# Gated cross-attention and a fake-quantised FFN on one core: the place of four weight chunks in VectorE's order, the queue of the raw up stores, and the place of one half of transposes

## The chip, the core and the metric

The kernel runs on one NeuronCore of a Trainium2 chip. Its engines work side by side, each through its own instructions in a fixed order: TensorE (PE: matmuls and transposes, with its weight loads shown as PEld), VectorE (DVE), ScalarE (ACT), GpSimd (POOL) and SyncE (SP, which only issues DMAs here). DMAs are issued through the queue of SP, ACT or POOL and are moved by 16 DMA engines. An instruction starts when it is at the head of its engine and what it waits for (semaphores) has happened.

The metric is the device time of one execution in microseconds (us). Before the change the median of three runs is 1495.26 us (1495.17 to 1497.37).

## The reference, cut to what matters

`x` has 4 x 1024 tokens of 512 channels, `ctx` 4 x 64 tokens. A layer norm and a cross-attention with 16 heads of 64 come first, then a layer norm and an FFN of width 1536, whose weights are quantised to 4 bits in blocks of 32 and whose activations are quantised to 16 bits with one scale for the whole tensor.

```python
x = x + jnp.tanh(g_xattn[0]) * xattn(_layernorm(x), ctx_1024, ctx_1024, w_q, w_k, w_v, w_o)
x = x + jnp.tanh(g_ffn[0]) * ffn(_layernorm(x), w_gate, w_up, w_down)

def ffn(x, w_gate, w_up, w_down):
    x = act_qdq(x)                          # 16 bits, one maximum over the whole tensor
    up = act_qdq(x @ lpbq_dequant(w_up).T)  # 4-bit weights, a scale for each block of 32
    gate = act_qdq(x @ lpbq_dequant(w_gate).T)
    sig = fixed_qdq_u16(jax.nn.sigmoid(gate))
    gate = act_qdq(gate * sig)
    o = act_qdq(gate * up)
    return o @ lpbq_dequant(w_down).T
```

Each `act_qdq` needs the maximum of a whole tensor before a single element can be rounded, so the FFN is cut into stages: all gate products, all up products, then the down products. Raw gate and raw up values go to memory in between.

## The kernel before, in words

**Stages.** (1) *Setup* (to about 95 us): the context is turned and multiplied with `w_k` and `w_v`, and `w_q`, `w_o` are folded in, so that attention needs only two products for each token tile: scores against `m_all`, weights against `vwo`. (2) *Attention* (95 to 580 us): 16 pairs of token tiles of 128. (3) *Gate products* (585 to 880 us), 24 units. (4) *Up products* (873 to 1180 us), 24 units. (5) *Down products* and output (1190 us to the end). The large products use Strassen's scheme: seven products m1 to m7 in place of eight, with the sums made on DVE and by accumulation in PSUM.

**Who sets the order.** In attention and in the gate and up stages PE runs in the order in which the code is written (`tc.manual_schedule`). The other engines' instructions are ordered by a planner from modelled costs; `tc.high_priority(SOON)` lets an instruction be drawn ahead, and `tc.keep_in_program_order(ins)` holds an instruction at its place in the code relative to others held so. An instruction that is not held may be placed far ahead of its place in the code.

**Setup.** `query_turned(hp)` turns `w_q` on PE (L443) and copies the result to `wqT` on DVE (L447). The products `ps_m` (L465) read `wqT`; their results are copied to `m_all` by ACT (L476) and DVE (L478). SP loads `c_sb`, `wk_sb`, `wq_sb`, `wv_sb`, `wo_sb`, the first token group `xg` and then four chunks `w_g`, in that order.

**Gate weights.** `dequantized` (L207 to L219) loads a chunk of 128 x 512, finds the largest magnitude of each block of 32 (L212, `wam`), makes scale and inverse (L213, L215), multiplies, rounds and multiplies back (L217, L218, L219). The twelve gate chunks are dequantised in the attention loop, each three tiles ahead (`AHEAD`) of the tile `gate_at` at which PE turns it (L224) inside `between`; the tile `wraw` has four buffers.

**Attention.** For pair q, `scores(q + 1)` and `softmax(q + 1)` are written first, then `attend(t)` for the two tiles of pair q. `softmax` runs 16 exponentials for each tile on ACT (L590) and normalises on DVE (L595, L596). `attend` turns the softmax tile in two halves of four transposes (L610, into PSUM `ps_e`), which ACT copies to `eT` (L612), calls `between` (a turned `xm` tile of an earlier group, L640, and at twelve tiles a gate chunk), then runs eight products `po` (L616): the first four read the first half of `eT`, the last four the second. `ps_e`, `ps_xm`, `ps_xn` and the turned weight chunks share the PSUM pool `ps_tr` of three buffers.

**Up stage.** Seven products of four matmul records each make a unit. `interleaved` sets PE's order to m1, m7 of the unit before, m5, m4 of the unit before, m2, m3 of the unit before, m6. m1 and m2 accumulate in the same PSUM bank `pp`: ACT must copy m1's result out (L766) before m2 may start, and m2's (L774) later. DVE takes the other results out (L779, L784, L944). `raw_up` has four buffers, two for each unit (`r0`, `r1`), so `r0` of a unit can be written only when the store of `r0` two units before has landed. `up_done` takes the maximum (L952) and stores the half unit to `up_d` (L956). ACT also makes the gate integers (L986, L987, L989) and magnitudes (L1018) there, DVE the products with them (L996, L1019).

Of the kernel before, what the change touches and what calls it, by code (L numbers as in the profile page):

```python
# [12 lines left out]
ALU = mybir.AluOpType  # L13
AX = mybir.AxisListType
# [3 lines left out]
P = 128  # L18
# [9 lines left out]
def kernel(  # L28
# [39 lines left out]
    nc = tc.nc  # L68
# [8 lines left out]
    TPB = S // P  # L77
# [12 lines left out]
    GRP = 4  # L90
# [113 lines left out]
            nc.vector.tensor_scalar(inv, inv, unit, None, ALU.mult)  # L204
        return s, inv

    def dequantized(pool, src, w, name):  # L207

        nc.sync.dma_start(out=w, in_=src)
        wb = w.rearrange("p (n k) -> p n k", k=QB)  # L210
        am = pool.tile([P, NQB], F32, name=f"wam_{name}", tag="wam")
        nc.vector.tensor_reduce(am, wb, AX.X, ALU.max, apply_absolute_value=True)  # L212
        nc.vector.tensor_scalar(am, am, 1.0 / W_QMAX, 1e-12, ALU.mult, ALU.max)  # L213
        inv = pool.tile([P, NQB], F32, name=f"winv_{name}", tag="winv")
        nc.vector.reciprocal(inv, am)  # L215
        shape = [P, NQB, QB]
        nc.vector.tensor_tensor(wb, wb, inv.unsqueeze(2).to_broadcast(shape), ALU.mult)  # L217
        nc.vector.tensor_scalar(w, w, MAGIC, MAGIC, ALU.add, ALU.subtract)  # L218
        nc.vector.tensor_tensor(wb, wb, am.unsqueeze(2).to_broadcast(shape), ALU.mult)  # L219
# [9 lines left out]
    wgT, wuT, wd, wdT, up_chunks = [], [], [], [], []  # L229

    def turned_chunk(psp, w, oc, into, name):

        if oc % 4 == 0:
            into.append(slot([P, HC, 4 * P], f"w{name}T{oc // 4}"))
        cols = slice((oc % 4) * P, (oc % 4 + 1) * P)
        ps = psp.tile([P, 4, P], F32, name=f"wps_{name}{oc}", tag="tr")
        turned(ps, w, into[-1][:, :, cols])
# [71 lines left out]
    pa = pools.enter_context(tc.tile_pool(name="pa", bufs=2))  # L309
    ps_tr = pools.enter_context(tc.tile_pool(name="ps_tr", bufs=3, space=PSUM))  # L310
# [52 lines left out]
    with tc.tile_pool(name="su", bufs=1) as su, tc.tile_pool(  # L363
        name="ps_mm", bufs=5, space=PSUM
# [7 lines left out]
        for k in range(P // BL):  # L372
            w = slice(k * BL, (k + 1) * BL)
# [77 lines left out]
        for hp in range(HP):  # L451
# [4 lines left out]
            for h2 in range(HC // 2):  # L456
# [13 lines left out]
                for j in range(2):  # L470
                    for b in range(B):
                        at = (hp % 4) * P + (j if b % 2 == 0 else 1 - j) * D
                        dst = m_all[b][hp // 4][:, 2 * h2 : 2 * h2 + 2, at : at + D]
                        src = two[j][:, :, b * KL : (b + 1) * KL]
# [43 lines left out]
    with tc.tile_pool(name="ps_s", bufs=1, space=PSUM) as ps_s, tc.tile_pool(  # L518
# [48 lines left out]
        def softmax(q, e):  # L567

            for i in range(2):
                t = 2 * q + i  # L570
                ei = e[:, i]

                if t % TPB == 0:
                    nc.vector.tensor_tensor(
                        ei, ei, cmask.unsqueeze(1).to_broadcast([P, NH, KL]), ALU.add
                    )
                mx = pa.tile([P, NH], F32, name=f"mx{t}", tag="mx")
                nc.vector.tensor_reduce(mx, ei, AX.X, ALU.max)
                sm = pa.tile([P, NH], F32, name=f"sm{t}", tag="sm")
                if q == 0:  # L580

                    nc.vector.tensor_tensor(
                        ei, ei, mx.unsqueeze(2).to_broadcast([P, NH, KL]), ALU.subtract
                    )
                    nc.scalar.activation(ei, ei, AF.Exp)
                    nc.vector.tensor_reduce(sm, ei, AX.X, ALU.add)
                else:
                    nc.vector.tensor_scalar(mx, mx, -1.0, None, ALU.mult)  # L588
                    for h in range(NH):
                        nc.scalar.activation(  # L590
                            ei[:, h, :], ei[:, h, :], AF.Exp, bias=mx[:, h : h + 1],
                            accum_out=sm[:, h : h + 1],
                        )
                rs = pa.tile([P, NH], F32, name=f"rs{t}", tag="rs")
                nc.vector.reciprocal(rs, sm)  # L595
                nc.vector.tensor_tensor(  # L596
                    ei, ei, rs.unsqueeze(2).to_broadcast([P, NH, KL]), ALU.mult
                )

        def attend(t, e, then):  # L600

            b = t // TPB
            g, i = divmod(t, GRP)
            ef = e[:, t % 2].rearrange("p h k -> p (h k)")
            eT = pa.tile([P, HP, P], F32, name=f"eT{t}", tag="eT")
            for q in range(HP // 4):
                ps = ps_tr.tile([P, 4, P], F32, name=f"ps_e{t}_{q}", tag="tr")
                for j in range(4):
                    hp = 4 * q + j
                    nc.tensor.transpose(ps[:, j, :], ef[:, hp * P : (hp + 1) * P], ident)  # L610
                with tc.high_priority(SOON):
                    nc.scalar.copy(eT[:, 4 * q : 4 * q + 4, :], ps)  # L612
            then()
            po = ps_o.tile([P, H], F32, name=f"po{t}", tag="po")
            for hp in range(HP):
                nc.tensor.matmul(  # L616
                    po, eT[:, hp, :], vwo[b][hp // 4][:, hp % 4, :],
                    start=(hp == 0), stop=(hp == HP - 1),
                )
            x1 = xg[g][:, i, :]  # L620
            with tc.high_priority(SOON):
                nc.vector.scalar_tensor_tensor(x1, po, tanh_g[0], x1, ALU.mult, ALU.add)
            nc.gpsimd.dma_start(out=x1_d[t], in_=x1)
            stats(pa, x1, mv2[:, t, :], f"b{t}")
# [30 lines left out]
        gate_raw = {}  # L655
# [10 lines left out]
        for q in range(NQ):  # L666
            b, k = divmod(q, QPB)
            e = ahead
            if q % 2 == 0 and q // 2 + 2 < NG:
                load_group(q // 2 + 2)  # L670

            if b + 1 < B:
                if b > 0 and k == 0:
                    fetched(m_all[b + 1], m_d[b + 1], f"mb{b + 1}")
                if b > 0 and k == QPB - 1:
                    fetched(vwo[b + 1], vwo_d[b + 1], f"vb{b + 1}")
                if k == 1:
                    sums_ahead = score_sums(b + 1)
                if k in (1, 2):
                    next(sums_ahead)  # L680
            if q + 2 < NQ:
                two = centred(q + 2)
            if q + 1 < NQ:
                ahead = scores(q + 1, lambda: next_left(q + 2))
                softmax(q + 1, ahead)
            for i in range(2):
                t = 2 * q + i

                def between():
                    if q > 1:  # L690
                        renormed(t - GRP)
                    if t in gate_at:
                        oc = gate_at.index(t)
                        turned_chunk(ps_tr, gate_raw.pop(oc), oc, wgT, "g")

                attend(t, e, between)
                if t + AHEAD in gate_at:
                    oc = gate_at.index(t + AHEAD)
                    w = pa.tile([P, H], F32, name=f"w_g{oc}", tag="wraw", bufs=4)
                    dequantized(pa, w_gate[oc * P : (oc + 1) * P, :], w, f"g{oc}")  # L700
                    gate_raw[oc] = w
                if t >= NT - UPB:
                    ag.append(weight_sums(wgT, sg_t, t - (NT - UPB), "g"))

                if t >= last - GRP:
                    oc = t - (last - GRP)
                    if oc % GRP == 0:
                        w4 = slot([P, GRP, H], f"w_eu{oc // GRP}")
                    w = w4[:, oc % GRP, :]
                    dequantized(pa, w_up[oc * P : (oc + 1) * P, :], w, f"eu{oc}")  # L710
                    early_up.append(w)
                for c, d in ((0, 2), (2, 3), (3, 4)):
                    if t == last + d - 1:
                        w = slice(last + c, last + d)
                        rstd_of(pa, [(rstd2[:, w], mv2[:, w, 1])], f"c{c}")
            if q % 2 == 1 and q + 1 < NQ:
                g = q // 2
                parts = [(rstd2[:, of_group(g)], mv2[:, of_group(g), 1])]
                if g + 2 < NG:
                    group_stats(pa, g + 2)  # L720
                    parts.append((rstd1[:, of_group(g + 2)], mv1[:, of_group(g + 2), 1]))
                rstd_of(pa, parts, f"b{g}")
# [12 lines left out]
    with tc.tile_pool(name="praw", bufs=RAW) as praw, tc.tile_pool(  # L735
# [184 lines left out]
        with tc.tile_pool(name="pc", bufs=2) as pc, tc.tile_pool(  # L920
# [27 lines left out]
            def up_done(r, v, k):  # L948
                u = unit_of(v, k)
                raw[u] = r.rearrange("p i n -> p (i n)")  # L950
                if v != order[-1]:
                    nc.vector.tensor_reduce(  # L952
                        am_up[:, u : u + 1], raw[u], AX.X, ALU.max, apply_absolute_value=True
                    )
                queue = nc.sync if v == order[-1] else nc.scalar
                queue.dma_start(out=up_d[u], in_=raw[u])  # L956


# [462 lines left out]
```

## Time and profile before

| | |
|---|---|
| median of three runs | 1495.26 us |
| the profiled execution: its time / its span | 1494.27 us / 1492.5 us |
| PE busy | 1444.5 us, 97% of the span |
| DVE, ACT, POOL busy | 1087.2, 635.6, 70.5 us |
| PE, one product of the up stage (two matmuls of 512 columns, four records) | starts every 1.72 us |
| raw up stores, 46 of 512 KB through ACT's queue (L956) | 338 ns of the queue each, landing after 2.6 / 4.9 / 8.5 us (least, median, most) |

The page lists busy time by engine, the span in 40 slices, the DMA queues, the chain of work that ended last, the costliest groups of instructions, and the DMA issues. The trace behind it answers for a stretch of time: what ran (the timeline, with the idle time ahead of an instruction and what ended it in brackets), who waited for whom, and busy time by window. A duration is in us in the timeline and in ns in lists by line; "x4" counts records.

### The profile page before, as it was taken

The numbers are of one execution on the slowest core, as the hardware profiler recorded it, in microseconds if no ns is written. First come the engines' busy times: TensorE is split into PE (matmuls) and PEld (weight loads), VectorE is DVE, ScalarE is ACT, GpSimd is POOL, SyncE is SP. The second block draws the span as 40 slices with busy tenths as digits, with TensorE's granted clock in tenths as the row PEclk, the third lists the DMA queues.
The fourth block names the chain that finished last, engine by engine and source line by source line (L and its number), as shares of the span: only waits on it lengthen the run. The fifth ranks groups of instructions, "written<-read, shape, count | busy, mean of one in ns | idle before, by whom it ended". The sixth has DMA issues, their size and how long they took to land. (4 is left out here: it accounts for less than half of the span.)

```text
span 1492.5 us, 14450 instructions
## 1 busy us (share of the span) xinstructions
PE 1444.5 (97%) x4656; PEld 795.4 (53%) x4656; DVE 1087.2 (73%) x1986; ACT 635.6 (43%) x1653; POOL 70.5 (5%) x143
## 2 busy tenths in 40 slices
PE   5999999999999999999999999999998899999999
PEld 4734444455445445444444444444443448888887
DVE  2777657567686978999855558888887897666642
ACT  0435566456655664110000127777789532222200
POOL 0000000000000001000000000000000101111110
PEclk8999999999999999999999999999999999999999
DMA  8250202311221234743322528858575485555321
GB/s 295 86 226 15 98 22 100 108 69 53 75 106 64 71 134 162 281 169 155 127 84 85 175 93 310 333 198 324 208 288 210 181 306 206 183 183 170 141 71 43
DMA packets 71475, 231.66 MB, mean 155 GB/s; under 512 B 7268, under 2 KB 7524, under 8 KB 65892
## 3 DMA queue, kind: packets, MB, share of 16 engines
q1 hardware_dynamic: 46212, 131.09, 24.7%
q0 software_dynamic: 11648, 50.34, 8.8%
q10 hardware_dynamic: 13536, 49.29, 8.3%
q8 instruction: 36, 0.59, 0.2%
q14 instruction: 43, 0.35, 0.1%
HBM read 123.74 MB, written 106.95 MB: 155 GB/s over the span
## 5 line engine op out<-in xcount | busy, mean ns | idle before, releaser
L590 ACT ACTIVATE e<-e,mx 128x64 f32<-128x64 f32 x480 | 159.6, 337 | 17.9 <-DVE mx L588 17.8
L616 PE MATMUL po<-vwo,eT 128*128 128x512 f32 x256 | 114.1, 599 | 2.3 <-ACT eT L612 2.0
L616 PE MATMUL po<-vb,eT 128*128 128x512 f32 x256 | 112.9, 594 | 0.8 <-ACT eT L612 0.8
L758 PE MATMUL pqup<-t,wuT 128*128 128x512 f32 x192 | 92.1, 602 | 2.2 <-DVE raw_up L779 1.7
L590 ACT ACTIVATION_READ_ACCUMULATOR e<-e,mx 128x1 f32 x480 | 91.6, 191 | 0.0
L758 PE MATMUL pqgate<-t,wgT 128*128 128x512 f32 x192 | 90.4, 593 | 0.0
L616 PEld LDWEIGHTS po<-vwo,eT 128*128 128x128 f32 x256 | 47.3, 190 | 58.8 <-issue 53.6
L1287 PE MATMUL ep<-wdT,upe 128*128 128x256 f32 x336 | 77.1, 379 | 0.0
L774 ACT COPY raw_gate<-ppgate 128x512 f32<-128x512 f32 x24 | 14.0, 585 | 147.8 <-PE ppgate L758 147.8
L616 PEld LDWEIGHTS po<-vb,eT 128*128 128x128 f32 x256 | 47.4, 190 | 55.2 <-issue 53.6
L1213 ACT ACTIVATE uie<-upe,inv_up 128x1024 int16<-128x1024 f32 x48 | 53.6, 1144 | 50.5 <-DVE upe L1217 31.5
L1287 PE MATMUL eq<-tw,upe 128*128 128x256 f32 x312 | 72.6, 380 | 0.5 <-DVE c L1305 0.5
L758 PE MATMUL ppup<-xu,wuT 128*128 128x512 f32 x144 | 69.2, 604 | 4.0 <-ACT raw_up L766 4.0
L1287 PEld LDWEIGHTS ep<-wdT,upe 128*128 128x128 f32 x336 | 63.8, 190 | 9.1 <-issue 0.5
L758 PE MATMUL ppgate<-xh,wgT 128*128 128x512 f32 x144 | 67.7, 592 | 0.0
L1217 DVE SCALAR_TENSOR_TENSOR upe<-uie,inv_o,gse 128x1024 f32<-128x1024 int16 (+1 forms) x50 | 60.5, 1237 | 5.3 <-ACT uie L1213 5.3
L1287 PEld LDWEIGHTS eq<-tw,upe 128*128 128x128 f32 x312 | 59.1, 190 | 9.1 <-DVE c L1305 1.1
L540 DVE TENSOR_TENSOR e<-sq,e 128x512 f32<-128x512 f32 x48 | 33.1, 689 | 42.1 <-PE sq L534 42.0
L758 PEld LDWEIGHTS pqup<-t,wuT 128*128 128x128 f32 x192 | 34.9, 189 | 52.1 <-issue 34.0
L758 PEld LDWEIGHTS pqgate<-t,wgT 128*128 128x128 f32 x192 | 36.2, 190 | 46.4 <-issue 38.5
L996 DVE SCALAR_TENSOR_TENSOR q<-gi,inv_gs,si 128x1024 int16<-128x1024 int16 x44 | 55.7, 1277 | 4.8 <-ACT si L989 4.7
L886 DVE TENSOR_REDUCE am_gate<-raw_gate 128x1 f32<-128x1024 f32 x48 | 58.2, 1212 | 0.9
(329 smaller groups left out, 2845.9 us busy)
## 6 DMA issues: line engine op xcount, KB each, us to landing
gate_d<-raw_gate ACTq DMA_DIRECT2D x48, 512.0 KB, 2.6
gt<-gate_d SPq DMA_DIRECT2D x48, 512.0 KB, 6.0
upe<-up_d SPq DMA_DIRECT2D x24, 1024.0 KB, 6.5
up_d<-raw_up ACTq DMA_DIRECT2D x46, 512.0 KB, 5.0
gse<-gsi_d SPq DMA_DIRECT2D x24, 512.0 KB, 5.0
gsi_d<-q SPq DMA_DIRECT2D x44, 256.0 KB, 4.3
xg<-in_x_dram SPq DMA_DIRECT2D x8, 1024.0 KB, 6.4
x_d<-xg POOLq DMA_DIRECT2D x32, 256.0 KB, 2.3
```

The source lines that it names most:

```text
L540: nc.vector.tensor_tensor(dst, bank[at], other, add)
L590: nc.scalar.activation(ei[:, h, :], ei[:, h, :], AF.Exp, bias=mx[:, h : h + 1], accum_out=sm[:, h : h + 1],)
L616: nc.tensor.matmul(po, eT[:, hp, :], vwo[b][hp // 4][:, hp % 4, :], start=(hp == 0), stop=(hp == HP - 1),)
L758: nc.tensor.matmul(bank[at], a[k][:, h, :], b[k][:, h, :], start=start and h == 0, stop=h == HC // 2 - 1, skip_group_check=True,)
L774: nc.scalar.copy(r0[:, 0, :], bank["pp"])
L886: nc.vector.tensor_reduce(am_gate[:, u : u + 1], rf, AX.X, ALU.max, apply_absolute_value=True)
L996: nc.vector.scalar_tensor_tensor(gsi[u], gi, c_gs, si, ALU.mult, ALU.mult)
L1213: nc.scalar.activation(ui, up[:, i, :], AF.Copy, scale=inv_u)
L1217: ins = nc.vector.scalar_tensor_tensor(o[:, i, w], ui[:, w], c_o, gs[:, i, w], ALU.mult, ALU.mult)
L1287: nc.tensor.matmul(bank[at], a[u // 2][k][:, u % 2, q % 2, :], w_of[u // 2][k][:, u % 2, :], start=start and u == 0, stop=u == UPB - 1, sk ...
```

## The change

Three edits.

1. The first instruction (the reduction) of gate chunks 0 to 3 is held in program order in DVE's stream.
2. The stores of raw up go out through POOL's queue rather than ACT's; those of the last unit stay with SP.
3. `attend` is split. A generator `weights_turned` turns one half of a softmax tile per step. For a pair, the first half of the second tile is turned after `between`'s work of the first tile and in front of the first tile's products; its second half is turned where the whole tile was turned before.

```diff
-    def dequantized(pool, src, w, name):
+    def dequantized(pool, src, w, name, in_order=False):
...
-        nc.vector.tensor_reduce(am, wb, AX.X, ALU.max, apply_absolute_value=True)
+        ins = nc.vector.tensor_reduce(am, wb, AX.X, ALU.max, apply_absolute_value=True)
+        if in_order:
+            tc.keep_in_program_order(ins)
...
-        def attend(t, e, then):
-
-            b = t // TPB
-            g, i = divmod(t, GRP)
+        def weights_turned(t, e):
+
             ef = e[:, t % 2].rearrange("p h k -> p (h k)")
             eT = pa.tile([P, HP, P], F32, name=f"eT{t}", tag="eT")
             for q in range(HP // 4):
...
                 with tc.high_priority(SOON):
                     nc.scalar.copy(eT[:, 4 * q : 4 * q + 4, :], ps)
-            then()
+                yield eT
+
+        def attend(t, eT):
+
+            b = t // TPB
+            g, i = divmod(t, GRP)
             po = ps_o.tile([P, H], F32, name=f"po{t}", tag="po")
...
+            turns = [weights_turned(2 * q + i, e) for i in range(2)]
+            next(turns[0])
             for i in range(2):
                 t = 2 * q + i
-
-                def between():
-                    if q > 1:
-                        renormed(t - GRP)
-                    if t in gate_at:
-                        oc = gate_at.index(t)
-                        turned_chunk(ps_tr, gate_raw.pop(oc), oc, wgT, "g")
-
-                attend(t, e, between)
+                eT = next(turns[i])
+                if q > 1:
+                    renormed(t - GRP)
+                if t in gate_at:
+                    oc = gate_at.index(t)
+                    turned_chunk(ps_tr, gate_raw.pop(oc), oc, wgT, "g")
+                if i == 0:
+                    next(turns[1])
+                attend(t, eT)
...
-                    dequantized(pa, w_gate[oc * P : (oc + 1) * P, :], w, f"g{oc}")
+                    dequantized(pa, w_gate[oc * P : (oc + 1) * P, :], w, f"g{oc}", oc < 4)
...
-                queue = nc.sync if v == order[-1] else nc.scalar
+                queue = nc.sync if v == order[-1] else nc.gpsimd
```

Because the planner places everything that is not held, the three edits also change the order of many other DVE, ACT and SP instructions in attention and in the up stage. PE's order changes only by the moved transposes.

## The prediction

> **What bounds the kernel now.** First the page: PE is busy 1444.5 of 1492.5 us. A faster DVE, ACT or queue is worth only the 48 us in which PE stands still, or runs slowly after it. So I read who PE waited for, longest first (engine, line, releaser: us in all, times, longest):
>
> ```profile
> PE ps_m L465 <- DVE wqT L447: 15.4, 1, 15.4
> PE ps_c L413 <- DMA c_sb<-in_ctx_dram: 4.7, 1, 4.7
> PE ps_d L1364 <- DVE upe L1222: 4.5, 1, 4.5
> PE ppup L758 <- ACT raw_up L766: 4.0, 1, 4.0
> PE po L616 <- ACT eT L612: 2.8, 10, 0.5
> ```
>
> Rows 1, 4 and 5 are what the three edits touch. Row 1 is a single stop in the setup; the timelines of PE and DVE there show its cause (start, duration, in brackets the idle time before and who ended it):
>
> ```profile
> 23.87 1.04 PE L443 MATMUL ps_wq<-ident,wq_sb 128*128 128x128 f32 x8
> 40.31 3.48 PE L465 MATMUL ps_m<-kT,wqT 64*128 64x256 f32 x16 [15.40 <-DVE wqT L447]
> ...
> 44.30 2.00 PE L465 MATMUL ps_m<-kT,wqT 64*128 64x256 f32 x16
> ```
>
> ```profile
> 29.67 0.69 DVE L212 TENSOR_REDUCE wam_g<-w_g 128x16 f32<-128x512 f32 x1 [22.35 <-DMA w_g<-in_L_ffn_w_gate_dram]
> ...
> 38.87 0.69 DVE L219 TENSOR_TENSOR w_g<-w_g,wam_g 128x512 f32<-128x512 f32 x1
> 39.48 1.28 DVE L447 COPY wqT<-ps_wq 128x512 f32<-128x512 f32 x2
> ```
>
> PE has turned the first `wq` chunk at 24.4, but DVE is stuck at the head of its stream on gate chunk 0, last in SP's load order, until 29.67. It then works off four chunks, and only then copies `wqT`. The granted clock shows a second cost (windows: us, busy and count of PE, PEld, DVE, ACT, POOL, then clock, DMA share, GB/s):
>
> ```profile
> 25.00:40.00 15.00, 0.00 (x0) 0.00 (x0) 10.26 (x25) 0.00 (x0) 0.00 (x0) 0.66 0.42 154
> 40.00:42.00 2.00, 1.69 (x8) 1.56 (x10) 0.76 (x2) 0.00 (x0) 0.00 (x0) 0.50 0.00 0
> 50.00:60.00 10.00, 10.00 (x70) 8.01 (x70) 5.48 (x19) 4.25 (x18) 1.41 (x2) 1.00 0.38 117
> ```
>
> Row 4 is one stop in the up stage (PE, then ACT):
>
> ```profile
> 1122.43 1.88 PE L758 MATMUL pqup<-t,wuT 128*128 128x512 f32 x4
> 1128.26 3.30 PE L758 MATMUL ppup<-xu,wuT 128*128 128x512 f32 x4 [3.96 <-ACT raw_up L766]
> 1131.36 2.31 PE L758 MATMUL pnup<-b,su 128*128 128x512 f32 x4
> ```
>
> ```profile
> 1125.75 1.99 ACT L1018 ACTIVATE ar<-raw_up 128x1024 f32<-128x1024 f32 x2
> 1127.52 0.36 ACTq L956 DMA_DIRECT2D up_d<-raw_up  x1
> 1127.65 0.56 ACT L766 COPY raw_up<-ppup 128x512 f32<-128x512 f32 x1
> ```
>
> PE's next product needs a PSUM bank that ACT should have emptied; ACT is busy without a gap on other work that stands ahead of that copy.
>
> **Edit 1, the held chunks.** In the changed program's DVE order no gate instruction stands ahead of `wqT` any more; all 24 of them stand in attention. What was hidden behind PE's stop must now be early enough. `wqT` for the first head pair: transposes end at 24.4, copy 0.68 us, handover about 0.2 (as elsewhere between these engines), so `ps_m` starts near 25.3 instead of 40.31: **15.0 us**. The first 16 `ps_m` records took from 40.31 to 43.72, 3.41 us, the next 16 took 1.93 (44.30 to 46.23); with no stop the clock stays at 1.00: **1.5 us** more. Is anything else late at 25 us? By issue time plus landing time, `wv_sb` is there by 20.8, `wo_sb` by 26.2, `xg` by 28.9; they are needed at about 30, 61 and 46 on the new clock. The POOL stores and the SP load of the next `xg` hang on `m_all` and `wqT`, and move with them. So 16.5 us, between 15 and 17.
>
> The chunks' DVE work (29.67 to 39.48, 9.8 us in all) moves behind tiles 13, 14, 15 and 17, about 290 to 375 us. From 300 to 400 DVE is busy 71.06 us and PE 99.49, so it has 29 us per 100 to take it. In the densest place two chunks' reductions and small steps, 1.7 us, stand between a tile's statistics and the first `sq` sum. DVE comes free about 1.7 us after `po` ends, that makes 3.4, and `sq` is due 3.6 us after `po` ends (two products of 1.72). Between this sum and the next stand 3.2 us where 3.4 are free. PE would wait only from 1.7 us later still (the product on `sn` lies between). Loss between 0 and 3; I take **0.5**. Each chunk is turned three tiles, some 40 us, after its reduction. Their DMAs keep their place in SP's queue.
>
> **Edit 3, the half turn.** No transposes are added. It puts 0.43 us of PE work between the first tile's second half and its products, and lets the second tile's products start on a half that is long copied. Row 5 is what it can remove: 10 stops of 0.18 to 0.46, 2.8 us, and 0.2 at `wps_g`. It adds a wait: at the eight even tiles from 16 on with a gate chunk, the moved half is the fifth in a row through three `ps_tr` buffers and needs the second half's copy. In the pair at 391.82 this copy ends at 393.58 (392.51 + 1.07) and the fifth transposes would start at 393.6: 0.1 to 0.2 each, 1.2 us in all. Queued behind it on PE are the eight products. It also needs the second tile's weights 3.4 us earlier than before; tightest is the last pair, with no scores ahead: normalised by 561.9, needed at about 562.7. Net between -1 and +3; I take **2.0**.
>
> **Edit 2, the stores.** It frees 46 x 0.338 = 15.5 us of ACT's queue and, worth more, ACT no longer stands still for DVE's sums before it issues. How late the stores were: DVE finished a half unit at 1112.95 and ACT's queue issued at 1116.81; the next was finished at 1116.45 and issued at 1124.00. And ACT's copies waited for such stores to land: 13.3 us, 6 times. POOL has no other work from the gate maximum to the last unit. Ideal length of the up stage: from 873.00, 24 x 7 products of 1.7165 = 288.4, three products of the gate tail 5.1, two transposed chunks 0.9: 294.4. Last product's end 1179.3, so 306.3 were taken and **11.9 are lost**. Of these 5.8 are the stop above (3.96, and 1.4 + 0.4 in the two slow products after it), 1.2 one slip at 1043.6, the rest slips of 0.1 to 0.2 where DVE's L779 is late.
>
> Does the stop go? Before it, 12 large ACT instructions of about 1.05 us stood between m2's copy at 1114.05 and m1's copy at 1127.65. In the changed program ACT's order is nearly the same in every unit: five between m1's copy and m2's (5.0 us; PE leaves 6.9), three between m2's and the next m1's (3.1; PE leaves 5.2); at the ends of the stage at most six and five. ACT needs about 9 us and DVE 9.4 of a unit's 12.0. So the stop and the slip, 7.0 us, should go. The small slips are DVE's order, which I leave in. Bounds: -2 to +11.9; I take **7.0**.
>
> Here a rule speaks against the edit. **The Trainium skill ("SBUF — State Buffer", section "SBUF: two separate sides")** says that descriptors of POOL's DMAs can't be written while DVE runs in a 2-port mode. Its figure: 0.62 us alone, 3.1 when overlapped. The row first:
>
> ```profile
> L623 POOL DMA_DIRECT2D x_d<-xg x32: 542/542/547, 132.4 to 579.2; - x32
> L867 POOL DMA_DIRECT2D ts_d<-t x12: 533/533/819, 589.7 to 734.6; - x12
> ```
>
> Under a DVE busy to 70 to 85% an issue took 533 to 547 ns and once 819; 256 KB landed after 2.3 us, 512 KB after 2.9. By the row a store costs 0.54 us on an idle engine; by the rule 2.5 us more. The room: `r0` is complete about 7.9 us into the next unit, and m1's copy of the second unit after it wants the buffer at 13.9: 5.9 us, and 4.6 more before PE stops, since m2 comes 5.15 us after m1. With the median landing of 4.9 the row gives no PE stop, and the rule (7.4) blocks ACT for 1.5 us per unit, still without one. I take the row: no cost.
>
> **Sum.** 16.5 + 2.0 + 7.0 - 0.5 = 25.0. The profiled execution took 1494.27 (span 1492.5 and 1.8 around it): 1469.3. The median of the runs lies 1.0 above it. I say **1470**.
>
> **Rivals.** (a) *The up stage gives nothing*: the new order of ACT and DVE trades the one stop for others as long (ACT copies late behind `ar`, which waits for DVE). For it: the whole stage is reordered, and DVE at 83% already slips. Against: the even order. 1494.3 - 18.0 = 1476. (b) *The up stage runs clean* and edit 3 gives its whole: 16.5 + 3 + 11.9, about 1463. (c) *The chunks' DVE work lands on PE*: if all 9.8 us stalled the scores, 1469.3 + 9.3 = 1479; against it, the slack of 1.7 us per sum. (d) *Slower*: POOL's stores starve. The place is m1's copy behind `r0`'s store. PE loses what a landing takes over 10.5 us after DVE's sum. To eat the 18 us that the other edits give, 22 units must lose 0.8 us each: every store must land after 11.3 us, where 8.5 is the worst seen. (e) *The edits don't do what they say*: the hold would have to leave the chunks in front, and the order excludes it.
>
> **Chances.** Forecast 0.60 (1465 to 1474), (a) 0.18, (b) 0.09, (c) 0.07, (d) 0.03, (e) and mishaps unseen 0.03. The range 1462.5 to 1481 takes in (b), (a), (c). About 0.2% (3 us) is what a measurement of this kernel tells from no change: faster 0.94, the same 0.02, slower 0.04.
>
> **What the profile after would show.** Right: `ps_m` starts near 25.3 with the clock at 1.00 to 60 us, and everything to 590 us lies 16 to 19 us earlier; PE's list has no row `ps_m` <- `wqT` and hardly one `po` <- `eT`; ACT's wait for `up_d` nearly gone, no stop of over 1 us between the first up product and the last, and the stage 7 us shorter. Wrong: PE waits for `e` L540 at 290 to 375 us (c); for `raw_up` L766 or L779 in the up stage (a); POOL issues over 1 us and landings of 8 us or more (d). The rows after 1190 us should keep their lengths.

## The result, and the profile after

The changed kernel takes **1473.72 us** (median of four runs, 1472.88 to 1474.68) against 1495.36 beside it: ratio 0.9853, 95% interval 0.9835 to 0.987, so some 22 us faster. Its profiled execution took 1473.96 us with a span of 1472.1, that is 20.3 us less than the one before.

The list of PE's waits of the changed kernel, as shown of before (engine, line, releaser: us in all, times, longest). It leaves out idle times under 0.15 us:

```profile
PE ps_c L415 <- DMA c_sb<-in_ctx_dram: 4.7, 1, 4.7
PE ps_xn L335 <- DVE xn L323: 3.2, 2, 2.6
PE ps_d L1371 <- SPq L1193: 2.7, 1, 2.7
PE pqup L765 <- DVE raw_up L786: 2.1, 4, 0.7
...
PE pqup L765 <- DVE raw_up L791: 1.8, 3, 1.2
...
PE ps_e L610 <- DVE e L598: 1.7, 2, 1.1
```

The three rows that the edits aimed at are gone from the top: `ps_m` <- `wqT` (15.4), `ppup` <- `raw_up` (4.0), `po` <- `eT` (2.8). In their place stand small waits for DVE: the normed tile `xn`, the sums of m6 (L786) and m7 (L791), the second tile's weights `e`.

PE's timeline in the setup (start, duration, in brackets the idle time before and who ended it), and the same three windows as before (us, busy and count of PE, PEld, DVE, ACT, POOL, then clock, DMA share, GB/s):

```profile
23.15 1.04 PE L445 MATMUL ps_wq<-ident,wq_sb 128*128 128x128 f32 x8
24.62 2.00 PE L467 MATMUL ps_m<-kT,wqT 64*128 64x256 f32 x16 [0.44 <-DVE wqT L449]
```

```profile
25.00:40.00 15.00, 15.00 (x103) 12.05 (x100) 8.95 (x36) 6.77 (x33) 0.95 (x2) 1.00 0.50 173
40.00:42.00 2.00, 2.00 (x13) 1.61 (x13) 0.21 (x1) 0.59 (x1) 0.47 (x1) 1.00 0.99 317
50.00:60.00 10.00, 9.29 (x63) 6.97 (x65) 9.51 (x34) 4.88 (x20) 1.06 (x2) 1.00 0.03 13
```

`ps_m` starts at 24.62 instead of 40.31, PE is busy all through 25 to 40 us, and the clock is 1.00 where it was 0.66 and 0.50. The setup went as predicted.

The up stage did not. PE and DVE, in the middle of it:

```profile
1028.00 1.88 PE L765 MATMUL ppup<-xu,wuT 128*128 128x512 f32 x4
1030.60 1.98 PE L765 MATMUL pqup<-t,wuT 128*128 128x512 f32 x4 [0.72 <-DVE raw_up L786]
```

```profile
1028.01 0.68 DVE L951 TENSOR_TENSOR raw_up<-pnup,raw_up 128x512 f32<-128x512 f32 x1
1028.73 1.22 DVE L959 TENSOR_REDUCE am_up<-raw_up 128x1 f32<-128x1024 f32 x1
1029.87 0.68 DVE L786 TENSOR_TENSOR raw_up<-pqup,raw_up 128x512 f32<-128x512 f32 x1
```

The first row is m1, the second m7 of the unit before, in the bank that m6 has filled. m7 may not start until DVE has taken m6's result out (L786), and DVE does that only after a maximum of 1.22 us (L959) that nobody waits for. The maximum stands directly in front of that sum in 18 of the 24 units; in the kernel before it did in 14. The wait shown is the longest of its kind; in most units m7 comes 0.25 us late.

Where the 20.3 us come from, by marks in the traces of before and after, and the same for the kernels of the experiments below. "Setup" ends at the first score product, "attention" at the first gate product; the up stage is from its first product to its last one's end, the gap from there to the first down product. All in us:

| kernel | setup | attention | gate | up | gap | median of runs | ratio to before, 95% interval |
|---|---|---|---|---|---|---|---|
| before | 95.6 | 490.6 | 286.8 | 306.5 | 10.9 | 1495.36 | |
| after | 78.4 | 489.7 | 286.8 | 305.0 | 10.2 | 1473.72 | 0.9853 [0.9835, 0.987] |
| edit 1 alone | 78.6 | 493.6 | 286.8 | 305.4 | 10.9 | 1481.01 | 0.99 [0.9883, 0.9916] |
| edit 2 alone | 96.4 | 490.6 | 286.8 | 303.9 | 10.2 | 1492.39 | 0.9974 [0.9964, 0.9984] |
| edit 3 alone | 96.4 | 485.4 | 286.8 | 306.4 | 10.9 | 1490.65 | 0.9962 [0.9948, 0.9976] |
| edits 1 and 3 | 79.0 | 488.0 | 286.8 | 307.8 | 10.9 | 1476.4 | 0.9868 [0.9852, 0.9885] |
| after, quiet chunks | 79.1 | 485.5 | 286.8 | 304.8 | 10.2 | 1470.15 | 0.983 [0.9817, 0.9844] |
| after, maximum deferred | 78.7 | 489.7 | 286.8 | 301.5 | 11.2 | 1471.54 | 0.9838 [0.9825, 0.9852] |
| both | 79.4 | 485.5 | 286.8 | 301.5 | 11.2 | 1468.11 | 0.9815 [0.9801, 0.9828] |

The gate stage, which no edit touches, keeps its length to 0.03 us in all of them. The setup varies by up to 1.0 between kernels of this table that share its code, so a difference of that size in one row means little. Each ratio is against runs of the kernel before on the same chip (medians 1495.35 to 1496.29).

### The profile page after: what moved, and what is told of

It reads as the page before. It is cut to its first block, busy times and chain, and to the rows that moved or that the text cites. A ratio compares the mean times of both kernels' runs of the same rounds, so it can differ in the third digit from the quotient of the medians.

```text
span 1472.1 us, 14498 instructions
## 1 busy us (share of the span) xinstructions
PE 1441.3 (98%) x4656; PEld 793.1 (54%) x4656; DVE 1090.3 (74%) x1986; ACT 639.4 (43%) x1653; POOL 95.5 (6%) x189
## 5 line engine op out<-in xcount | busy, mean ns | idle before, releaser
L993 ACT ACTIVATE gi<-gt,inv_gate 128x1024 int16<-128x1024 f32 x48 | 54.9, 1143 | 30.6 <-DVE q L1003 30.3
```

Source lines behind the costliest of these rows:

```text
L993: nc.scalar.activation(gi, g, AF.Copy, scale=inv_g)
```

## The experiments

### The edits one by one

Edit 1 alone (before, with these lines):

```diff
-        nc.vector.tensor_reduce(am, wb, AX.X, ALU.max, apply_absolute_value=True)
+        ins = nc.vector.tensor_reduce(am, wb, AX.X, ALU.max, apply_absolute_value=True)
+        if in_order:
+            tc.keep_in_program_order(ins)
...
+                    dequantized(pa, w_gate[oc * P : (oc + 1) * P, :], w, f"g{oc}", oc < 4)
```

> The kernel before with the held gate chunks alone. The prediction's terms: 16.5 from the setup less 0.5 for the chunks' work in attention, so 16.0 us faster, about 1479. Theory from the trace of after: attention starts 17.2 earlier, but the chunks' steps stand in front of the normed tile xn in the pairs that carry group statistics (first xn wait and the slow products after it, some 4.3 us), so about 13 us faster, 1482, with PE waits for xn of about 3 us in all, all between 290 and 380 us. Rival: the whole 9.8 us of chunk work lands on PE, 7 us faster, 1488, with waits spread over every one of the four chunks' tiles. The up stage should keep its length of 306.3 us and its 4 us stop for ACT's copy.

Measured: 1481.01, some 15 us faster, between the prediction's 16 and the trace reading's 13. The setup gained 17.0 and attention gave back 2.9, not 9.8 as the rival has it. The 4.0 us stop for ACT's copy stayed.

Edit 2 alone:

```diff
-                queue = nc.sync if v == order[-1] else nc.scalar
+                queue = nc.sync if v == order[-1] else nc.gpsimd
```

> The kernel before with the stores on POOL's queue alone. The prediction's term: 7.0 us faster, about 1488. Theory from the trace of after: the stop for ACT's copy goes (5.8 us) but the regular order of DVE puts the maximum of the second half unit in front of m6's sum, which PE needs, so nearly each unit slips 0.2 to 0.35 us; net 1.5 us in the up stage, about 1493.5, stage 304 to 306 us, with start to start distances of near 1.96 in place of 1.72 at m7 and most PE waits behind DVE's sums of m6 and m2. Rival: the slips come from the other edits (an up stage that starts at another phase), then the stage is near 299 us. Rival from the skill: stores block, an issue of over 1 us and ACT waits for landings.

Measured: 1492.39; by the interval 2.4 to 5.4 us faster, not 7.0. The stage is 303.9, and the waits that remain in it are those for L779 and L784, the sums of m6 and m7. Start to start, m7 and the product after it come 5.9 us late in the whole stage here and 6.9 in after, but 3.2 in before, 2.1 with edit 1 alone and 3.1 with edits 1 and 3. So these slips come with edit 2 itself and not with the other two edits.

Edit 3 alone (the split of `attend`, as in the diff of the change):

```diff
+                if i == 0:
+                    next(turns[1])
+                attend(t, eT)
```

> The kernel before with the half turn alone. The prediction's term: 2.0 us faster, about 1493. Theory from the trace of after: 3.0 us of waits go and each pair of tiles also gains 0.1 at each set of products (6.97 to 6.865 in a row of products), less 1.1 in the first pair, where the second tile's weights are now late: 4 to 5 us faster, about 1490.5, with no PE wait for eT and the start of the gate stage at about 581.5 instead of 586.2. Rival: the waits move to the turned half's bank (ps_tr) and nothing is gained, 1495.

Measured: 1490.65, 5.5 faster; attention 5.2 shorter, with no wait of `po` for `eT`. The prediction had 2.0. What it overlooked stands in the groups by line, in the rows of the weight loads (PEld), first of before, then of edit 3 alone (busy us, mean ns | idle before, who ended it):

```profile
L616 PEld LDWEIGHTS po<-vb,eT 128*128 128x128 f32 x256 | 47.4, 190 | 55.2 <-issue 53.6 <-ACT eT L612 1.5
L616 PEld LDWEIGHTS po<-vwo,eT 128*128 128x128 f32 x256 | 47.3, 190 | 58.8 <-issue 53.6 <-ACT eT L612 4.7
```

```profile
L621 PEld LDWEIGHTS po<-vb,eT 128*128 128x128 f32 x256 | 47.4, 190 | 53.6 <-issue 53.6
L621 PEld LDWEIGHTS po<-vwo,eT 128*128 128x128 f32 x256 | 47.4, 190 | 53.7 <-issue 53.6
```

The weight loads waited 6.2 us for `eT`, twice what the matmuls' row shows. Sixteen matmul records behind a late load took 7.13 us instead of 7.03 (20 of 32 tiles before, one with edit 3), 1.9 us in all: in PE's list that is busy time and not a wait. Start to start, the waits in front of the products come to 5.3 us before and to nothing with edit 3, more than the list's 2.8, which counts from modelled ends and leaves out the shortest. Some of this came back elsewhere in attention, 1.1 of it in the first pair.

Edits 1 and 3 without edit 2 (after, with the stores on ACT's queue again):

```diff
-                queue = nc.sync if v == order[-1] else nc.gpsimd
+                queue = nc.sync if v == order[-1] else nc.scalar
```

> The kernel after with the raw up stored through ACT's queue again (so the held chunks and the half turn, no change in the stores). If the three edits add up as the trace of after reads: 18.1 us before the gate stage and 0 after it, about 1477; the prediction's terms say 18.0, about 1477 too, so this run does not tell the two apart for attention, but it does tell what the stores give on top: after less this run is 1.5 to 2.5 us by the trace, 7 us by the prediction. Rival: the up stage's stop depends on the phase in which the stage starts and not on the stores; then it changes here too.

Measured: 1476.4. The 4.0 us stop for ACT's copy is back, as in all four kernels that store through ACT's queue, though the stage starts at four different times (854 to 873 us): the rival, by which the stop depends on that, is out. The up stage with the gap is 3.5 us longer than in after. Its attention is 1.7 us *shorter* than in after, though it has the same 2.6 us wait. PE's timeline at that wait, of after and of this run, and the clock around it:

```profile
341.46 1.31 PE L335 MATMUL ps_xn<-ident,xn 128*128 128x128 f32 x8 [2.61 <-DVE xn L323]
342.56 3.39 PE L536 MATMUL sn<-mb,xs 128*128 128x512 f32 x4
```

```profile
342.00:344.00 2.00, 2.00 (x7) 1.24 (x7) 1.85 (x5) 1.17 (x2) 0.00 (x0) 0.54 0.03 8
344.00:346.00 2.00, 2.00 (x5) 0.78 (x4) 0.79 (x3) 0.00 (x0) 0.00 (x0) 0.60 0.00 0
```

```profile
342.06 1.08 PE L335 MATMUL ps_xn<-ident,xn 128*128 128x128 f32 x8 [2.60 <-DVE xn L323]
342.98 1.88 PE L536 MATMUL sn<-mb,xs 128*128 128x512 f32 x4
```

```profile
342.00:344.00 2.00, 1.94 (x11) 1.46 (x12) 2.00 (x5) 1.07 (x2) 0.00 (x0) 1.00 0.03 8
344.00:346.00 2.00, 2.00 (x15) 1.41 (x13) 2.00 (x5) 0.61 (x2) 0.00 (x0) 1.00 0.00 0
```

The same stop let the clock fall to 0.54 and 0.60 in the one and left it at 1.00 in the other; the product behind it took 3.39 us or 1.88. So the stop costs 2.6 or about 4.3; the last section shows what decides it.

### What edit 1 costs in attention

DVE's timeline ahead of the 2.6 us wait, in after:

```profile
334.83 0.68 DVE L219 TENSOR_TENSOR w_g<-w_g,winv_g 128x512 f32<-128x512 f32 x1
...
335.56 0.42 DVE L220 TENSOR_SCALAR w_g<-w_g 128x512 f32<-128x512 f32 x1
...
336.49 0.68 DVE L221 TENSOR_TENSOR w_g<-w_g,wam_g 128x512 f32<-128x512 f32 x1
...
338.89 0.69 DVE L542 TENSOR_TENSOR e<-sq,e 128x512 f32<-128x512 f32 x1 [0.92 <-PE sq L536]
...
340.77 1.00 DVE L323 TENSOR_SCALAR xn<-xg,mv,rstd 128x512 f32<-128x512 f32 x2
```

A chunk's steps (L219 to L221) stand among the statistics from which `xn` is made. They delay these until the next score sum stands in front, on which DVE itself must wait (0.92); `xn` comes at 341. The test works the four held chunks off in pairs of tiles that make no `xn`:

```diff
+        made_at = [1, 5, 9, 13, *(t - AHEAD for t in gate_at[4:])]
...
-                if t + AHEAD in gate_at:
-                    oc = gate_at.index(t + AHEAD)
+                if t in made_at:
+                    oc = made_at.index(t)
```

> The kernel after with the four held chunks worked off by DVE one by one behind tiles 1, 5, 9 and 13, each in a pair of tiles that carries no group statistics, where DVE has no normed tile to make; the chunks are turned where they were. If the chunks' steps in front of xn are what cost attention: the waits for xn at 341 us go and about 4 us with them, 1469.5. If the loss at 341 us comes from something else (the statistics themselves, already there before, or the clock), same as after, 1473.7. If the 2 us between the first and second score sums can't hide a chunk, waits appear at the score sums in four pairs, up to 1 us each, and the gain is 0 to 2.

Measured: 1470.15, 3.6 below after. Of PE's waits for `xn` one of 0.6 is left, which edit 3 alone has too, and attention takes 485.5, as with edit 3 alone (485.4). So the held chunks cost 2.5 to 4.2 us in attention (4.2 where the clock fell) because of where they stood, and nothing in quiet pairs.

### What holds the up stage

The maximum of the second half unit is put behind m6's sum, and both are held:

```diff
+            while later:
+                tc.keep_in_program_order(later.pop(0)())
             tail[:] = rest
...
-                    nc.vector.tensor_tensor(r1[:, 0, :], bank["pq"], r0[:, 1, :], add)
+                    ins = nc.vector.tensor_tensor(r1[:, 0, :], bank["pq"], r0[:, 1, :], add)
+                if name == "up":
+                    tc.keep_in_program_order(ins)
...
+                    if k == 1:
+                        later.append(largest)
+                    else:
+                        largest()
```

> The kernel after with one change in DVE's order in the up stage: the maximum of the second half unit (1.22 us) stands behind the sum of m6 of the following unit instead of in front of it. If that maximum is what delays PE by 0.2 to 0.35 us in nearly every unit: 23 units, 5 to 8 us faster, about 1467, stage 297 to 300 us, start to start distances at m7 back at 1.72. If PE is held by DVE's whole load in the unit (83 to 88% busy), the wait moves to the sum of m2 or of m3 and little is gained, 0 to 2 us. The second half's store is not delayed by it.

> The kernel after with both of the last two changes: chunks in quiet pairs and the maximum behind m6's sum. Each acts in its own stage, so they should add: 4 plus 5 to 8, 1462 to 1465. If the second only moves the wait, 1469.5.

Measured: 1471.54 and, with the quiet chunks, 1468.11. The stage is 3.5 us shorter, the gap behind it 1.0 longer: 2.5 where 5 to 8 were expected. From PE's waits for sums of DVE in the deferred version:

```profile
PE pqup L765 <- DVE raw_up L793: 3.1, 6, 1.0
...
PE pqup L765 <- DVE raw_up L786: 0.3, 1, 0.3
```

The wait for m6's sum is nearly gone, but much of it came back at m7's (L793), which m4 needs. In after, PE loses 5.0 us from m1 to m7 (23 distances of 44.52 us in all, against 23 x 1.7165) and 1.8 in m7 itself, 0.1 a time; with the maximum deferred the two come to 0.4. In exchange m4 and the product after it come 5.3 us late in all, where it was 1.2.

Is it order, or DVE's load? The maxima of the second half units are left out, zeros put in their place:

```diff
-                if v != order[-1]:
+                if v != order[-1] and k == 1:
+                    nc.gpsimd.memset(am_up[:, u : u + 1], 0.0)
+                elif v != order[-1]:
```

> The kernel after without the maxima of the second half units in the up stage (22 x 1.22 us of DVE's work left out; zeros are put in their columns by POOL). It bounds what DVE's work in front of m7 and m4 costs. If it is only where that maximum stands, leaving it out gives about what deferring it gave, 2.5 to 3.5 us against after. If DVE's load is the limit of the stage, it gives clearly more: up to the whole loss of 10 us, so 6 to 10 us, with no wait of PE for DVE's sums between the first unit and the last.

Measured: 1478.09, *slower* than after, which neither theory had. Time by four units, from m1 to m1 (28 products of 1.7165 would take 48.06 us):

| | units 1-4 | 5-8 | 9-12 | 13-16 | 17-20 |
|---|---|---|---|---|---|
| before | 48.44 | 48.52 | 49.00 | 49.98 | 48.34 |
| after | 49.27 | 49.03 | 50.11 | 50.11 | 49.47 |
| maximum deferred | 49.37 | 48.94 | 49.76 | 49.11 | 48.42 |
| maximum left out | 49.42 | 56.73 | 50.15 | 48.58 | 48.07 |

In the second four units something jammed. ACT, then DVE, in the run with the maximum left out:

```profile
938.74 0.59 ACT L773 COPY raw_up<-ppup 128x512 f32<-128x512 f32 x1 [4.34 <-DMA up_d<-raw_up]
```

```profile
942.39 1.29 DVE L1005 SCALAR_TENSOR_TENSOR q<-gi,inv_gs,si 128x1024 int16<-128x1024 int16 x1 [6.18 <-ACT si L998]
```

A store landed late (5.8 to 10.5 us around there, as gate and token loads ran beside it), ACT's copy stood still for it and held back ACT's integers, and DVE, at the head of its stream, waited 6.2 us for these with PE's sums queued behind. Leaving work out changed the planner's order as well; it isn't a clean experiment for the whole stage. In the last column it is: DVE's order there is that of after without the maximum, and the time is 0.01 us from the ideal, against 1.4 in after and 0.4 with the maximum deferred. In those four units the maximum is the whole loss, and most of it is its place. For the columns in front of it, where 2.1 and 0.5 us are lost even without the maximum, the share of DVE's load stays open.

One integer product per unit is moved behind m7's sums, which are held (on top of both earlier changes):

```diff
+                if k == 0:
+                    while ints:
+                        tc.keep_in_program_order(ints.pop(0)())
...
+                    ins = nc.vector.tensor_tensor(r1[:, 1, :], bank["pq"], r0[:, 1, :], add)
+                    if name == "up":
+                        tc.keep_in_program_order(ins)
```

> The kernel with quiet chunks and the deferred maximum, and one integer product of DVE per unit (1.28 us) moved behind m7's sums, so that m7's sum, which the product m4 waits for, stands 1.28 us earlier in DVE's stream. If the waits left in the up stage (2.8 us for m7's sum, five times) are order alone, they go: 2 to 3 us faster, about 1465.5. If they come of DVE's load or of the few buffers behind it, they move to m4's or m6's sum and the time is the same or up to 2 us longer.

Measured: 1487.43, ratio 0.9945 [0.9931, 0.9958], 19 us worse than without it. PE's waits for m7's sum came to 17.6 us, where they were 2.8 with both earlier changes. The longest of them, and the last DVE instruction in front of the sum that ends it:

```profile
1115.96 3.78 PE L766 MATMUL pqup<-t,wuT 128*128 128x512 f32 x4 [9.57 <-DVE raw_up L794]
```

```profile
1114.02 1.28 DVE L1023 SCALAR_TENSOR_TENSOR last_q<-gi,inv_gs,si 128x1024 int16<-128x1024 int16 x1 [3.49 <-ACT si L1014]
```

Near the end the code makes several integer products in a row; two of them waited 3.5 us each for ACT, and m7's sum, now held, stood behind them. This test says nothing on whether the remaining waits are order or load.

### The queue, and the first pair

```diff
-                queue = nc.sync if v == order[-1] else nc.gpsimd
+                queue = nc.sync
```

> The kernel after with the raw up stored through SP's queue instead of POOL's. DVE's order in the up stage is that of after. If what edit 2 brings is ACT freed of the stores, whatever queue takes them, this is the same as after within 1.5 us. If POOL's issues are held up by DVE, this is faster. Rival: SP issues in order, so a store that waits for DVE's sum holds back the loads of gates and tokens behind it; then ACT waits for gate loads and the time is 3 us or more above after.

> The kernel with quiet chunks and the deferred maximum, and the raw up stored through SP's queue. With SP the stores landed sooner (3.1 us against 3.5) and the up stage of the plain version was 1.7 us shorter. If that is the queue: about 1.5 us faster than with POOL, 1466.5. If it was only the chance of where the slips fall, 1468 again; if the two act on the same slips (those in front of m7), 1467.5 to 1468.

Measured: 1472.09 (ratio 0.9842, 0.9827 to 0.9858) in place of after's 1473.72, and 1466.66 (0.9813, 0.9799 to 0.9826) with the other two changes, in place of 1468.11. Both intervals overlap those with POOL: what edit 2 brings is ACT freed of the stores, whichever of the two queues takes them. Whether SP's is worth the 1.5 us stays open. 1466.66 is the lowest median seen.

The half turn only from the second pair on:

```diff
-                if i == 0:
+                if i == 0 and soon:
                     next(turns[1])
```

> The kernel with quiet chunks and the deferred maximum, and the half turn only from the second pair of tiles on. In the first pair the second tile's weights are not ready when its half is to be turned (1.1 us of PE waits at its ps_e). If that wait is lost time: 1.1 us faster, about 1467. If the wait only comes back at the second tile's own turn, where the weights are as late for PE: no change, 1468.

Measured: 1468.95, ratio 0.982 [0.9806, 0.9833]; no different from 1468.11. The 1.1 us wait at the first pair's `ps_e` went from the list, and attention was 0.3 us shorter: most of it came back elsewhere.

## Why the prediction came out as it did

It said 1470, with 1465 to 1474 for its own case; the time is 1473.7, just inside. That it is inside is in part luck: edit 3 gave 3.2 more than its term, which nearly covered the 3.7 that the chunks lost beyond theirs.

- **Edit 1, the setup: right.** 16.5 was said and 17.2 is the difference of the two traces (17.0 with edit 1 alone); `ps_m` at 24.6 where 25.3 was said. The cold clock went with the stop.
- **Edit 1, the chunks in attention: too small.** The term was 0.5; edit 1 alone and the pair of edits 1 and 3 show 2.5 to 2.9, and after 4.2, of which 1.7 are the fallen clock. The step that failed is the slack: it was counted at the score sums, 1.7 us a sum, and the late instruction was `xn`, whose transposes come between two score products and which I had not checked. Rival (c), with all chunk work on PE (9.8), is too large.
- **Edit 3: too small.** 2.0 was taken from PE's list of waits for `eT`; 5.2 is what edit 3 alone gives, because weight loads waited 6.2 us for the same copies. The wait that I added for the fifth half in three buffers (1.2) did not come: at the eight places the half's first transpose starts 0.11 us after the chunk's last, as transposes do in a row. The weights of the last pair, named as the tightest place, were on time, and those of the first pair late by 1.1.
- **Edit 2: the term that failed, 7.0.** The up stage gained 1.5 and the gap behind it 0.7 against before; alone, edit 2 gained 2.6 and 0.7. The stop and the slow products behind it went, as said: 6.7 us by the starts of the 168 products. But m7 and the product after it came 3.6 us later than before in all, m4 0.6 and the last unit's end 1.0. So the step that failed is "the small slips are DVE's order, which I leave in", which put a change of that order at nothing. The table by four units shows after 0.5 to 1.1 us above before in four of the five columns.

  The slip at 1043.6, counted among the 7.0, did not go either: it is the wait at 1030.60 shown above, 0.9 us where it was 1.25; with edit 1 alone it was 0.15, so it does not hang on the queue. I had read evenness as good in itself, and had counted ACT's instructions between copies but not DVE's between the sums.

  The maximum's place alone is not the whole difference: it stood in front of m6's sum in 14 units before, which lost 2.4 us in all from m1 to m7, and stands there in 18 in after, which lost 4.3 of the 5.0. DVE also comes to it later: it begins m6's sum more than 1.05 us behind the start of m1 in 17 units in after, and in 7 before. What in the new order makes it so late was tested only by the maximum. Rival (a), which named this trade, was nearer for the stage than the forecast.
- **The rule on POOL's stores: the row held.** The stores of after (groups by line):

```profile
L963 POOL DMA_DIRECT2D up_d<-raw_up x46 | 24.5, 533 | 258.3 <-ACT si L996 100.8 <-DVE raw_up L951 77.3 <-ACT gi L993 31.6
```

  They took 533 ns each, under a DVE that is busy for 237 of 276 us there; the 46 stores landed after 3.6 us in the median, where it was 5.0, and ACT's waits for landings fell from 13.3 to 7.3 us. So nothing was blocked here; whether DVE ran in a mode to which the rule applies, no run shows. Rival (d) did not come about. Its mechanism is real all the same: with the maximum left out, late landings started the jam.

Of the forecast's sum of 25.0, 20.3 arrived in the profiled execution: +0.7 from the setup, -0.6 in attention (3.2 more from edit 3, less 3.7 more lost to the chunks) and -4.8 in the up stage with the gap behind it.

## What to carry to other kernels

When an edit frees a planner to lay an engine's stream out anew, list per period which instruction on it somebody waits for and what now stands in front of that instruction; an even order repeats its one bad place period after period. Work pushed out of an idle stretch should be put by hand where its engine has nothing due, and the slack is to be checked at each thing that engine makes there. Waits of the weight loads belong to a product's cost as much as those of its matmuls.

## What the runs showed of the hardware

- **A stop of 2.6 us was enough for the clock to fall, but not each time, and what decides it is where the stop lies on a fixed grid.** Six kernels have after's placing of the chunks, and all have the stop, 2.60 to 2.84 us long. In each trace every recorded change of the granted clock lies a whole multiple of 3.413 us from the others. In after the stop lies from 338.85 to 341.46, wholly inside the stretch from 338.77 to 342.18, and the clock is 0.50 in the stretch behind it, to 345.59. So it is with SP's queue (2.60 us of the stop inside one stretch), with the maximum left out (2.54) and with the maximum deferred (2.27). With edit 1 alone and with edits 1 and 3 the stop is cut by the grid into 0.90 and 1.93 us, and 0.76 and 1.84, and the clock stayed at 1.00. The Trainium skill ("TensorE: Matmul & The Clock Gate", section "What's actually happening") has a free-running window of about 3.4 us behind the clock; these traces agree, and show that a stop shorter than the window can do it. One such stretch at half the clock costs 1.7 us, which is the difference in attention between after and edits 1 and 3, though the two have the same code there: a difference of that size between two kernels can be the phase of the grid alone. It may differ between executions of one kernel too: of after's four, the one with a mean clock of 0.999 has the shortest span, 1470.4 against 1471.5 to 1472.9 at 0.996 to 0.997. No trace of it was kept.
- **A late weight load shows as a longer product.** Sixteen `po` records took 7.13 us with a late load and 7.03 without, and the idle time that PE's list put down to these waits (2.8 us) was half of what the loads had waited (6.2).
